# A graph network's attention steps on one core: weight pieces staged in pairs, late rows' parts asked for earlier, a difference moved to VectorE

## The chip, the core and the metric

The kernel runs on one core of one Trainium2 chip. The core has a matrix engine (TensorE, PE in the profile, with its weight loads as PEld), VectorE (DVE), ScalarE (ACT), GpSimd (POOL) and SyncE (SP), whose queue issues most DMAs. The metric is the time of one execution on the device in microseconds, the median of several runs. The profile is of one further execution.

## What is computed

1024 nodes of 512 features, 16 graphs of 64 nodes with 256 condition vectors each, 4 layers of attention and a gated feed-forward part between two graph convolutions:

```python
def _attn(xf, cond, Wq, Wk, Wv, Wo):
    q = (xb @ Wq).reshape(BS, -1, H, DH)
    k = (cond @ Wk).reshape(BS, -1, H, DH)
    v = (cond @ Wv).reshape(BS, -1, H, DH)
    att = jnp.einsum('bnhd,bmhd->bhnm', q, k) * DH ** (-0.5)
    w = jax.nn.softmax(att, axis=-1)
    o = jnp.einsum('bhnm,bmhd->bnhd', w, v).reshape(BS, -1, H * DH)
    return (o @ Wo).reshape(n, d)
...
h = (x - mu) * jax.lax.rsqrt(var + EPS) * bn_w + bn_b
h = _gcn(h, src, dst, gcn_in_w, gcn_in_b, n)
for i in range(L):
    a = _attn(_ln(h, ln2_w[i], ln2_b[i]), cond, Wq[i], Wk[i], Wv[i], Wo[i])
    h = h + a
    u = _ln(h, ln3_w[i], ln3_b[i]) @ geglu_w[i] + geglu_b[i]
    val, gate = jnp.split(u, 2, axis=-1)
    f = val * jax.nn.gelu(gate, approximate=False)
    h = h + f @ ffo_w[i] + ffo_b[i]
h = _gcn(h, src, dst, gcn_out_w, gcn_out_b, n)
return h + x_in
```

## The kernel before

**Products in three parts.** Large products are made of operands with few bits. An operand x is split in three: a high part (x scaled, rounded by ScalarE), a low part (what is left, by VectorE) and a third, their difference (by VectorE or GpSimd). A unit of a product (class `Twelve`, L352) is twelve matmuls of 128 by 512 into one PSUM bank: `begin` runs high by high and low by low, eight matmuls, and then ScalarE multiplies the bank in place (L373); `end` adds the four matmuls of the third parts and copies the bank out (L378 on VectorE, L380 on ScalarE). Units are staggered: another unit begins between a unit's `begin` and its `end`, so that ScalarE has that long for its scaling. There are eight PSUM banks.

**The attention loop** (from L1659) runs g over six of a layer's eight pairs of graphs. In a step the four key units of pair g + 1 run first, then the probabilities of pair g are transposed (`mix`, L882) and multiplied with its values (`po`, L866), while the first value unit of pair g + 1 begins; ScalarE writes the high part `oh` of the result (L890). Then come the scores of pair g + 1 (L823), their maxima on VectorE (L832), the exponentials on ScalarE (L843), the remaining value units, and the output product of pair g (`attn_out`, L904). Layer 0 also transposes and splits the condition blocks; later layers load their parts (`load_parts`, L283).

**Staged weights.** During these steps `staged(l)` (L943) prepares weight columns for the feed-forward part. It handles four column blocks j. Each is loaded (`fetch`, into tiles of a pool of six, of which the output weights hold four) and divided into pieces of 128 by 256: four for j = 0 and 1, seven sums and differences for j = 2 and 3. `stage` (L934) sends a piece through a staging buffer: high part on ScalarE (L938), low and third on VectorE (L939, L940), and a store to DRAM (L941). There are two such buffers (tag `gs2`). `staged` is a generator; each `next(staging)` in the loop places its next stretch at that point, behind all that ScalarE and VectorE have been given so far (`behind_traced`). Before the change a stretch is a whole block of four pieces, or three and four of the seven, at up to three places per step: behind the second key unit's begin, behind the first value unit's end, and at the end of step 3.

**The start of the feed-forward part** (from L1774). The rows of the last two pairs of graphs come late. Their normalised rows are transposed (L1844, L1845), written by both VectorE (L808) and ScalarE (L810), and then split (`split_late`, `split_right`, L1749 to L1761) for the second half of the plain columns (`half_1`). `ln3_sums` (L1605 to L1607) and `ln3_last_sum` (L1612) make sums and differences of row blocks for a Strassen-like scheme, whose parts follow in `late_parts` (L1861 to L1866). `ready[0]` is the first staged chunk: `begin_first` and `end_first` make its first product, `steps` the others, with sums on VectorE (L1160, L1185).

Within an engine the order is fixed when the program is built; names in rows such as `gs2_1_2_5` read: tile, layer 1, column block 2, piece 5. `k_1_5_2` is key unit 2 of layer 1's pair 5.

Of the kernel before, what the change touches and what calls it, by code (L numbers as in the profile page):

```python
# [18 lines left out]
P = 128  # L19
# [7 lines left out]
def gnn_kernel(  # L27
# [26 lines left out]
    nc = tc.nc  # L54
# [888 lines left out]
    def staged(l):  # L943
# [16 lines left out]
            return [of[:, i * M:(i + 1) * M] for of in tiles for i in range(2)]  # L960

        def split(j, pieces):
            if j < 2:
                for k, x in enumerate(pieces):
                    stage(x, half_dram[j, k], f"{l}_{j}_{k}")
                yield
                return
            a11, a21, a12, a22 = pieces
            name = f"{l}_{j}"
            s1, s2 = (rows.tile([P, M], F32, tag="gy", name=f"gy{i}_{name}", bufs=2)  # L970
                      for i in range(2))

            def put(x, i):
                stage(x, chunk_dram[j - PLAIN, SPLIT.index(i)], f"{name}_{i}")

            nc.vector.tensor_tensor(s1, a21, a22, OP.add)
            put(a22, 3)
            nc.vector.tensor_tensor(s2, s1, a11, OP.subtract)
            put(s1, 4)
            nc.vector.tensor_tensor(a21, a11, a21, OP.subtract)  # L980
            put(a11, 0)
            yield
            put(a21, 6)
            put(a12, 1)
            nc.vector.tensor_tensor(a12, a12, s2, OP.subtract)
            put(s2, 5)
            put(a12, 2)
            yield

        for j in range(KC):  # L990
            pieces = fetch(j)
            yield
            flow = split(j, pieces)
            for some in range(1 if j < PLAIN else 2):
                if some:
                    yield
                with behind_traced(mybir.EngineType.DVE, mybir.EngineType.Activation):
                    next(flow)

    class HalfWeights:  # L1000

# [490 lines left out]
    for l in range(L):  # L1492
# [103 lines left out]
        def ln3_turn(nb, by=(0, 1), each=lambda ins: ins):  # L1596
            turn(xns.pop(nb), ln3T[nb // 4], nb % 4 * P, LN3W + l * KC, LN3B + l * KC,
                 f"ln3_{l}_{nb}", by, each)
# [60 lines left out]
        for g in range(NG - 2):  # L1659
# [7 lines left out]
            for i, u in enumerate(k):  # L1667
                u.begin()
                if not i:
                    for end in ends:  # L1670
                        end()
                if i > 1:
                    k[i - 2].end()
                if i == 1 and g > 2:
                    next(staging, None)
                next(wo_flow, None)
            k[-2].end()
            for _ in wo_flow:
# [14 lines left out]
                split_cond(g + 2, None if g else scores.last)  # L1693
            v[1].begin()
            v[0].end()
            if g in (2, 3, 4):
                next(staging)
            v[2].begin()
            v[1].end()
            pieces = attn_out(l, g, oT, wo, pin)  # L1700
# [10 lines left out]
                scale_kept()  # L1711
            if l == 0 and g + 3 < NG:
                turn_cond(g + 3, each=pin)
            if g == 3:
                next(staging)
            if g == NG - 3:
                add_bias(nc.vector, *range(4))
# [50 lines left out]
        def split_late(at):  # L1768
            flows = [split_right(i, x, at) for i, x in late]
            for _ in range(2):  # L1770
                for flow in flows:
                    next(flow, None)
# [42 lines left out]
        with in_order(mybir.EngineType.DVE):  # L1815
# [27 lines left out]
            units[3].begin()  # L1843
            ln3_turn(g - 1, (1, 1), pin)  # L1844
            ln3_turn(g, (0, 0), pin)  # L1845
            units[2].end()
            ready[0].begin_first()
            units[3].end()
            split_late(slice(2 * P, 4 * P))
            ready[0].begin(1)  # L1850
            ready[0].end_first()
            ln3_sums(nc.vector, g - 1, g)
            ln3_last_sum(nc.gpsimd, g - 3, g - 2)
            ln3_last_sum(nc.gpsimd, g - 1, g)
        Chunk.rights[2] = rights[2]
# [29 lines left out]
        def fill(n=1):  # L1885
            for _ in range(n):
                next(parts, None)

        units = half_1(0) + half_1(1)
        units[0].begin()  # L1890
        fill(3)
        units[1].begin()
        units[0].end()
# [228 lines left out]
```

## Time and profile before

| | us |
|---|---|
| median of 3 runs | 2274.92 |
| lowest and highest run | 2270.91, 2276.71 |
| the profiled execution, its whole time | 2275.67 |
| the profiled execution, its span | 2273.9 |
| busy: VectorE, ScalarE, GpSimd | 1718.2, 1156.8, 506.6 |

The mean granted clock of TensorE in that execution is 0.997 of full speed. A row of the timeline has the start in us from the span's start, the time to the end of the row's last instruction, the engine, the line, the operation, the tiles written and read, the shapes, the count, and in brackets the idle time before it with what ended it. A row of the list of waits has who waited for whom, and then the total in us, the number of waits and the longest. A row of a window has its bounds, its length, the busy time of each engine with its number of instructions, the granted clock, the DMA share and GB/s. SPq is SP's DMA queue.

### The profile page before, as it was taken

What the parts mean: (1) busy time and instruction counts of PE and PEld (TensorE: products, weight loads), DVE (VectorE), ACT (ScalarE), POOL (GpSimd) and SP (SyncE); (2) the same over time, 40 slices, a digit from 0 to 9 for tenths busy, and PEclk for the clock granted to TensorE, in tenths of its full rate; (3) what the DMA queues carried; (4) which work ended last, traced back from release to release, by engine and by line L of the source; (5) the groups of instructions that cost most, each with busy time, mean ns of one, the idle gap of its engine ahead of it and who ended that gap; (6) DMA issues with size and microseconds to landing.
All of it is one profiled execution on the core that took longest, in us unless ns stands there. A gap on an engine that the chain in (4) does not pass through costs nothing. (4 is left out here: it accounts for less than half of the span.)

```text
span 2273.9 us, 35755 instructions
## 1 busy us (share of the span) xinstructions
PE 2240.1 (99%) x12768; PEld 1809.2 (80%) x12768; DVE 1718.2 (76%) x3296; ACT 1156.8 (51%) x2313; POOL 506.6 (22%) x487
## 2 busy tenths in 40 slices
PE   8999999999999999999999999999999999999999
PEld 5678878887888878888888887878888887878787
DVE  9886577999965466899975456899976466899965
ACT  7555555565354445565345445555436445566521
POOL 1122101485000000287000000178100000068301
PEclk9999999999999999999999999999999999999999
DMA  6154564434525264443534265443543346353551
GB/s 171 57 185 167 188 217 166 144 121 148 166 79 191 87 250 158 146 127 98 192 120 169 93 211 182 128 146 103 182 161 135 126 158 216 112 165 111 181 183 54
DMA packets 216953, 340.84 MB, mean 150 GB/s; under 512 B 16488, under 2 KB 117168, under 8 KB 216768
## 3 DMA queue, kind: packets, MB, share of 16 engines
q1 hardware_dynamic: 214672, 333.05, 43.2%
q0 software_dynamic: 1376, 4.30, 0.5%
q8 instruction: 105, 1.72, 0.3%
q10 hardware_dynamic: 720, 1.11, 0.1%
q14 instruction: 80, 0.66, 0.1%
HBM read 236.69 MB, written 101.72 MB: 149 GB/s over the span
## 5 line engine op out<-in xcount | busy, mean ns | idle before, releaser
L1154 ACT ACTIVATE g<-g 128x512 f32<-128x512 f32 x224 | 131.3, 586 | 185.9 <-PE g L1140 183.7
L1612 POOL TENSOR_TENSOR ln3T<-ln3T,ln3T 128x512 f32<-128x512 f32 x8 | 13.2, 1650 | 892.2 <-DVE ln3S L1605 892.2
L1319 PE MATMUL fy<-bl_wff,al_f 128*128 128x512 f32 x512 | 158.8, 390 | 0.0
L1319 PE MATMUL fx<-bs_wff,as_f 128*128 128x512 f32 x512 | 158.6, 390 | 0.0
L1319 PE MATMUL fy<-bh_wff,ah_f 128*128 128x512 f32 x512 | 157.7, 389 | 0.0
L304 ACT ACTIVATE ah_f<-fr 128x1024 fp32r<-128x1024 f32 x64 | 67.8, 1060 | 173.0 <-DVE al_f L305 81.7
L373 ACT ACTIVATE k<-k 128x512 f32<-128x512 f32 x125 | 73.1, 586 | 157.9 <-PE k L362 157.6
L843 ACT ACTIVATE pr<-sc,nmax 128x256 f32<-128x256 f32 x256 | 118.4, 473 | 40.6 <-DVE nmax L832 40.5
L832 DVE TENSOR_REDUCE nmax<-sc 128x2 f32<-128x512 f32 x128 | 83.6, 678 | 70.6 <-PE sc L823 70.6
L373 ACT ACTIVATE v<-v 128x512 f32<-128x512 f32 x127 | 74.7, 588 | 111.8 <-PE v L362 111.8
L1084 POOL TENSOR_TENSOR gsa<-gha,gla 128x512 fp32r<-128x512 f32 x96 | 122.6, 1299 | 19.8 <-DVE gla L1079 19.8
L1140 PE MATMUL g<-gr,gha 128*128 128x512 f32 x384 | 118.2, 389 | 0.0
L362 PE MATMUL v<-bs_wv,cs 128*128 128x512 f32 x384 | 104.6, 396 | 8.9 <-ACT v L373 8.9
L1319 PEld LDWEIGHTS fy<-bl_wff,al_f 128*128 128x128 f32 x512 | 96.1, 188 | 21.7 <-DVE bl_wff L1296 1.7
L1319 PEld LDWEIGHTS fx<-bs_wff,as_f 128*128 128x128 f32 x512 | 96.1, 188 | 21.4 <-DVE bs_wff L1300 1.7
L1319 PEld LDWEIGHTS fy<-bh_wff,ah_f 128*128 128x128 f32 x512 | 96.1, 188 | 19.8
L362 PE MATMUL v<-bh_wv,ch 128*128 128x512 f32 x384 | 107.9, 403 | 0.0
L362 PE MATMUL k<-ch,bh_wk 128*128 128x512 f32 x384 | 104.0, 393 | 0.0
L305 DVE SCALAR_TENSOR_TENSOR al_f<-ah_f,fr 128x1024 fp32r<-128x1024 f32 x64 | 78.1, 1221 | 34.2 <-ACT ah_f L304 28.1
L362 PE MATMUL v<-bl_wv,cl 128*128 128x512 f32 x384 | 103.2, 390 | 0.0
L362 PE MATMUL k<-cl,bl_wk 128*128 128x512 f32 x384 | 102.8, 389 | 0.0
L362 PE MATMUL k<-cs,bs_wk 128*128 128x512 f32 x384 | 101.4, 395 | 0.0
(333 smaller groups left out, 5951.4 us busy)
## 6 DMA issues: line engine op xcount, KB each, us to landing
f_dram<-fT SPq DMA_DIRECT2D x128, 256.0 KB, 2.1
fr<-f_dram SPq DMA_DIRECT2D x64, 512.0 KB, 4.6
ch<-cond_dram SPq DMA_DIRECT2D x48, 512.0 KB, 4.7
cl<-cond_dram SPq DMA_DIRECT2D x48, 512.0 KB, 6.2
cs<-cond_dram SPq DMA_DIRECT2D x48, 512.0 KB, 7.3
chunk_dram<-gs SPq DMA_DIRECT2D x56, 384.0 KB, 2.6
wff<-in_L_gnn_ffo_w_dram SPq DMA_DIRECT2D x32, 512.0 KB, 5.3
half_dram<-gs SPq DMA_DIRECT2D x32, 384.0 KB, 2.9
```

Of the source, the lines that this page charges most:

```text
L304: nc.scalar.mul(twelve_bits(h), x, INWARD * TINY)
L305: left_parts.low = nc.vector.scalar_tensor_tensor(twelve_bits(l), h, -1.0 / TINY, x, OP.mult, OP.add)
L362: pin(nc.tensor.matmul(self.bank, twelve_bits(left[k // 2])[:, k % 2, self.c * P:(self.c + 1) * P], twelve_bits(right[k // 2])[:, k % 2, : ...
L373: nc.scalar.mul(self.bank, self.bank, 1.0 + TINY)
L832: nc.vector.tensor_reduce(nmax[u], banks[u].rearrange("p (a m) -> p a m", a=2), AX.X, OP.max, negate=True)
L843: nc.scalar.activation(pr3[:, a, :], ps3[:, a, :], AF.Exp, bias=nmax[u][:, a:a + 1], accum_out=tot[:, a:a + 1])
L1084: split_left.last = pin(t.tensor_tensor(s_at, h_at, l_at, OP.subtract))
L1140: pin(nc.tensor.matmul(to, self.part(i, which)[:, k, :], self.rights[i][which].bitcast(F32R)[:, k, :], start=start and k == 0, stop=stop a ...
L1154: pin(nc.scalar.mul(to, to, 1.0 + TINY))
L1319: pin(nc.tensor.matmul(to, twelve_bits(left[which][0])[:, k, b * P:(b + 1) * P], twelve_bits(right[which])[:, k, :], start=u == 0 and whic ...
L1612: t.tensor_tensor(b12, b22, b12, OP.subtract)
```

## The change

Three edits, in every layer:

- `staged` gives its pieces in pairs (`islice(flow, 2)`), at four places of a step: behind the begin of the second and of the fourth key unit, behind the first value unit's end, and at the step's end. The 22 pieces of a layer now start at the end of step 2 and end in step 5. Each pair's arithmetic is otherwise the same; within blocks 2 and 3 the sums stand beside the pieces that they serve.
- `split_late` for the late rows stands right behind the last transposes instead of behind the last unit of the first half; `end_first` stands behind the begin of the second half's first unit.
- the late rows' third difference (`ln3_sums`, third) is made on VectorE instead of GpSimd.

```diff
@@ -960,10 +960,10 @@
             return [of[:, i * M:(i + 1) * M] for of in tiles for i in range(2)]
 
         def split(j, pieces):
-            if j < 2:
+            if j < PLAIN:
                 for k, x in enumerate(pieces):
                     stage(x, half_dram[j, k], f"{l}_{j}_{k}")
-                yield
+                    yield
                 return
             a11, a21, a12, a22 = pieces
             name = f"{l}_{j}"
@@ -975,27 +975,30 @@
 
             nc.vector.tensor_tensor(s1, a21, a22, OP.add)
             put(a22, 3)
+            yield
+            put(s1, 4)
+            yield
             nc.vector.tensor_tensor(s2, s1, a11, OP.subtract)
-            put(s1, 4)
             nc.vector.tensor_tensor(a21, a11, a21, OP.subtract)
             put(a11, 0)
             yield
             put(a21, 6)
+            yield
             put(a12, 1)
+            yield
             nc.vector.tensor_tensor(a12, a12, s2, OP.subtract)
             put(s2, 5)
+            yield
             put(a12, 2)
             yield
 
         for j in range(KC):
-            pieces = fetch(j)
-            yield
-            flow = split(j, pieces)
-            for some in range(1 if j < PLAIN else 2):
-                if some:
-                    yield
+            flow = split(j, fetch(j))
+            for _ in range(2 if j < PLAIN else 4):
+                yield
                 with behind_traced(mybir.EngineType.DVE, mybir.EngineType.Activation):
-                    next(flow)
+                    for _ in islice(flow, 2):
+                        pass
 
     class HalfWeights:
 
@@ -1671,8 +1674,8 @@
                         end()
                 if i > 1:
                     k[i - 2].end()
-                if i == 1 and g > 2:
-                    next(staging, None)
+                if i % 2 and g > 2:
+                    next(staging)
                 next(wo_flow, None)
             k[-2].end()
             for _ in wo_flow:
@@ -1693,8 +1696,8 @@
                 split_cond(g + 2, None if g else scores.last)
             v[1].begin()
             v[0].end()
-            if g in (2, 3, 4):
-                next(staging)
+            if g > 1:
+                next(staging, None)
             v[2].begin()
             v[1].end()
             pieces = attn_out(l, g, oT, wo, pin)
@@ -1711,7 +1714,7 @@
                 scale_kept()
             if l == 0 and g + 3 < NG:
                 turn_cond(g + 3, each=pin)
-            if g == 3:
+            if 1 < g < NG - 3:
                 next(staging)
             if g == NG - 3:
                 add_bias(nc.vector, *range(4))
@@ -1843,13 +1846,12 @@
             units[3].begin()
             ln3_turn(g - 1, (1, 1), pin)
             ln3_turn(g, (0, 0), pin)
+            split_late(slice(2 * P, 4 * P))
             units[2].end()
             ready[0].begin_first()
             units[3].end()
-            split_late(slice(2 * P, 4 * P))
             ready[0].begin(1)
-            ready[0].end_first()
-            ln3_sums(nc.vector, g - 1, g)
+            ln3_sums(nc.vector, g - 1, g, third=nc.vector)
             ln3_last_sum(nc.gpsimd, g - 3, g - 2)
             ln3_last_sum(nc.gpsimd, g - 1, g)
         Chunk.rights[2] = rights[2]
@@ -1888,6 +1890,7 @@
 
         units = half_1(0) + half_1(1)
         units[0].begin()
+        ready[0].end_first()
         fill(3)
         units[1].begin()
         units[0].end()
```

ScalarE in layer 1, from the copy of the keys in step 4 to the exponentials of pair 5, before the change:

```order
L380 COPY kT_1_5_1_22492<-k_1_5_2_22477 128x512
L882 COPY pT_1_4_0_22532<-tr_pr_1_4_0_22527 128x512
L938 ACTIVATE gs2_1_2_1_22455<-gx_1_2_1_22348 128x256
L882 COPY pT_1_4_2_22546<-tr_pr_1_4_2_22541 128x512
L938 ACTIVATE gs2_1_2_5_22461<-gy1_1_2_22406 128x256
L373 ACTIVATE v_1_5_0_22560<-v_1_5_0_22560 128x512
L938 ACTIVATE gs2_1_2_2_22466<-gx_1_2_1_22348 128x256
L890 ACTIVATE oh_1_4_22602<-po_1_4_22526 128x512
L843 ACTIVATE pr_1_5_0_22630,tot_1_5_0_22631<-sc_1_5_0_22606,nmax_1_5_0_22626 128x256 x2
```

The same place of the changed kernel, from just behind that copy:

```order
L938 ACTIVATE gs2_1_2_5_22493<-gy1_1_2_22406 128x256
L882 COPY pT_1_4_0_22521<-tr_pr_1_4_0_22516 128x512
L882 COPY pT_1_4_2_22535<-tr_pr_1_4_2_22530 128x512
L373 ACTIVATE v_1_5_0_22549<-v_1_5_0_22549 128x512
L890 ACTIVATE oh_1_4_22591<-po_1_4_22515 128x512
L843 ACTIVATE pr_1_5_0_22619,tot_1_5_0_22620<-sc_1_5_0_22595,nmax_1_5_0_22615 128x256 x2
L843 ACTIVATE pr_1_5_1_22629,tot_1_5_1_22630<-sc_1_5_1_22596,nmax_1_5_1_22617 128x256 x2
L843 ACTIVATE pr_1_5_2_22639,tot_1_5_2_22640<-sc_1_5_2_22597,nmax_1_5_2_22625 128x256 x2
L843 ACTIVATE pr_1_5_3_22647,tot_1_5_3_22648<-sc_1_5_3_22598,nmax_1_5_3_22635 128x256 x2
L373 ACTIVATE v_1_5_1_22657<-v_1_5_1_22657 128x512
L380 COPY v_1_5_0_22671<-v_1_5_0_22549 128x512
L938 ACTIVATE gs2_1_2_2_22674<-gx_1_2_1_22348 128x256
```

Pieces 1, 5 and 2 of block 2 stood between the key copy and `oh`; now piece 5 alone stands there, ahead of the transposed probabilities, and piece 2 behind the exponentials; piece 1 stands ahead of the key copy, outside these rows.

VectorE in layer 1 at the late rows, before the change:

```order
L808 TENSOR_SCALAR ln3T_1_1_1_23098<-tr_ln3_1_6_23690,cols_85 128x128 x2
L1047 SCALAR_TENSOR_TENSOR fT_1_0_1_23723<-g0_1_0_1_23680,gcols_86,gg_1_0_1_23475 128x512
L1751 SCALAR_TENSOR_TENSOR gr_1_7_1_23469<-ln3T_1_1_0_23097,gr_1_7_0_23468 128x2x256
L1751 SCALAR_TENSOR_TENSOR gr_1_2_1_23472<-ln3T_1_1_1_23098,gr_1_2_0_23471 128x2x256
L1761 SCALAR_TENSOR_TENSOR gr_1_7_2_23470<-gr_1_7_0_23468,gr_1_7_1_23469 128x2x256
L1761 SCALAR_TENSOR_TENSOR gr_1_2_2_23473<-gr_1_2_0_23471,gr_1_2_1_23472 128x2x256
L1605 TENSOR_TENSOR ln3S_1_0_23099<-ln3T_1_1_0_23097,ln3T_1_0_0_23095 128x2x256
L1606 TENSOR_TENSOR ln3S_1_1_23100<-ln3T_1_1_1_23098,ln3S_1_0_23099 128x2x256
L1864 SCALAR_TENSOR_TENSOR gl_1_5_23760<-ln3S_1_1_23100,gr_1_5_23758 128x512
```

The same place of the changed kernel:

```order
L808 TENSOR_SCALAR ln3T_1_1_1_23098<-tr_ln3_1_6_23690,cols_85 128x128 x2
L1754 SCALAR_TENSOR_TENSOR gr_1_7_1_23469<-ln3T_1_1_0_23097,gr_1_7_0_23468 128x2x256
L1754 SCALAR_TENSOR_TENSOR gr_1_2_1_23472<-ln3T_1_1_1_23098,gr_1_2_0_23471 128x2x256
L1764 SCALAR_TENSOR_TENSOR gr_1_7_2_23470<-gr_1_7_0_23468,gr_1_7_1_23469 128x2x256
L1764 SCALAR_TENSOR_TENSOR gr_1_2_2_23473<-gr_1_2_0_23471,gr_1_2_1_23472 128x2x256
L1050 SCALAR_TENSOR_TENSOR fT_1_0_1_23729<-g0_1_0_1_23680,gcols_86,gg_1_0_1_23475 128x512
L1608 TENSOR_TENSOR ln3S_1_0_23099<-ln3T_1_1_0_23097,ln3T_1_0_0_23095 128x2x256
L1609 TENSOR_TENSOR ln3S_1_1_23100<-ln3T_1_1_1_23098,ln3S_1_0_23099 128x2x256
L1610 TENSOR_TENSOR ln3S_1_2_23101<-ln3T_1_0_1_23096,ln3S_1_1_23100 128x2x256
L1866 SCALAR_TENSOR_TENSOR gl_1_5_23760<-ln3S_1_1_23100,gr_1_5_23758 128x512
```

The four instructions of the late parts stand ahead of the product `fT` of the last unit, and the difference `ln3S_1_2` has come in behind the other two sums.

ScalarE in layer 1 at the second half's first units, before the change:

```order
L1177 COPY gs1_1_0_2_23737<-g0_1_0_2_23713 128x512
L373 ACTIVATE g1_1_1_0_23748<-g1_1_1_0_23748 128x512
L1861 ACTIVATE gr_1_5_23758<-ln3S_1_1_23100 128x512 x2
L373 ACTIVATE g0_1_1_0_23772<-g0_1_1_0_23772 128x512
L1861 ACTIVATE gr_1_6_23767<-ln3T_1_1_0_23097 128x512 x2
L1044 ACTIVATE gg_1_1_0_23746<-g1_1_1_0_23748,gcols_86 128x512
L1861 ACTIVATE gr_1_23821<-ln3S_1_2_23101 128x512
L373 ACTIVATE g1_1_1_1_23804<-g1_1_1_1_23804 128x512
```

The same place of the changed kernel:

```order
L373 ACTIVATE g1_1_1_0_23744<-g1_1_1_0_23744 128x512
L1180 COPY gs1_1_0_2_23754<-g0_1_0_2_23719 128x512
L1863 ACTIVATE gr_1_5_23758<-ln3S_1_1_23100 128x512 x2
L1863 ACTIVATE gr_1_23821<-ln3S_1_2_23101 128x512
L1863 ACTIVATE gr_1_6_23767<-ln3T_1_1_0_23097 128x512 x2
L373 ACTIVATE g0_1_1_0_23772<-g0_1_1_0_23772 128x512
L1047 ACTIVATE gg_1_1_0_23742<-g1_1_1_0_23744,gcols_86 128x512
L1863 ACTIVATE gr_1_23821<-ln3S_1_2_23101 128x512
L1863 ACTIVATE gr_1_4_23791<-ln3S_1_0_23099 128x512 x2
L373 ACTIVATE g1_1_1_1_23804<-g1_1_1_1_23804 128x512
```

Five first parts of the late sums (`gr_1_5` twice, `gr_1`, `gr_1_6` twice) stand ahead of the scaling of the second unit (`g0_1_1_0`), where two stood.

## The prediction

> **What bounds the kernel now.** I read the page first, then the list of waits of TensorE, then its timeline at each wait, and last the timelines of the engines it waited for.
>
> ```profile
> span 2273.9 us, 35755 instructions
> PE 2240.1 (99%) x12768; PEld 1809.2 (80%) x12768; DVE 1718.2 (76%) x3296; ACT 1156.8 (51%) x2313; POOL 506.6 (22%) x487
> PE v L362 <- ACT v L373: 12.6, 6, 3.5
> PE g L1140 <- DVE g L1160: 2.7, 4, 0.8
> PE g L1140 <- DVE gl L1864: 0.4, 2, 0.2
> ```
>
> TensorE (PE) is busy for 2240.1 of 2273.9 us, so no other engine can give time back except by ending a wait of TensorE. The change touches no matmul's size, only orders. What it can win lies in three of these lines: 12.6 us in which the last third of a value unit waits for ScalarE to scale its bank (L373), and 2.7 + 0.4 us at the start of the feed-forward part, where TensorE waits for VectorE. The profiled execution took 2275.67 us, 1.8 us more than its span; the median of the three runs is 2274.92 us, 0.75 us below it. The sum is made against 2275.67.
>
> The wait rows hide a part of the loss, so I take whole steps of the attention loop. The first value matmuls behind the scores of step g + 1 mark one step each; layer 0 first, then 1, 2 and 3.
>
> ```profile
> 245.50 1.20 PE L362 MATMUL v<-bh_wv,ah_c 128*128 128x512 f32 x4
> 277.79 1.20 PE L362 MATMUL v<-bh_wv,ah_c 128*128 128x512 f32 x4
> 311.02 1.20 PE L362 MATMUL v<-bh_wv,ah_c 128*128 128x512 f32 x4
> 347.89 1.20 PE L362 MATMUL v<-bh_wv,ah_c 128*128 128x512 f32 x4
> 806.17 1.20 PE L362 MATMUL v<-bh_wv,ch 128*128 128x512 f32 x4
> 836.66 1.20 PE L362 MATMUL v<-bh_wv,ch 128*128 128x512 f32 x4
> 871.61 1.20 PE L362 MATMUL v<-bh_wv,ch 128*128 128x512 f32 x4
> 1359.92 1.20 PE L362 MATMUL v<-bh_wv,ch 128*128 128x512 f32 x4
> 1396.74 1.20 PE L362 MATMUL v<-bh_wv,ch 128*128 128x512 f32 x4
> 1886.02 1.20 PE L362 MATMUL v<-bh_wv,ch 128*128 128x512 f32 x4
> 1919.57 1.20 PE L362 MATMUL v<-bh_wv,ch 128*128 128x512 f32 x4
> ```
>
> An undisturbed step is 277.79 - 245.50 = 32.29 us in layer 0, which also transposes its condition blocks, and 836.66 - 806.17 = 30.49 us in layers 1 to 3. The step behind the scores of g = 5 is 36.87, 34.95, 36.82 and 33.55 us: **4.58, 4.46, 6.33 and 3.06 us too long, 18.43 us together**. Layer 0 also loses 0.94 us one step earlier (33.23 us).
>
> Why that step? ScalarE and VectorE in layer 1, in order of time:
>
> ```profile
> 823.32 0.42 ACT L938 ACTIVATE gs<-gx 128x256 fp32r<-128x256 f32 x1 [3.06 <-DMA gx<-in_L_gnn_geglu_w_dram]
> 827.58 0.42 ACT L938 ACTIVATE gs<-gx 128x256 fp32r<-128x256 f32 x1 [1.88 <-DMA chunk_dram<-gs]
> 829.61 0.59 ACT L882 COPY pT<-tr_pr 128x512 f32<-128x512 f32 x1
> 837.54 0.42 ACT L938 ACTIVATE gs<-gx 128x256 fp32r<-128x256 f32 x1 [2.50 <-DMA chunk_dram<-gs]
> 837.87 0.58 ACT L890 ACTIVATE oh<-po 128x512 fp32r<-128x512 f32 x1
> 838.79 1.28 DVE L832 TENSOR_REDUCE nmax<-sc 128x2 f32<-128x512 f32 x2
> 843.45 0.59 ACT L373 ACTIVATE v<-v 128x512 f32<-128x512 f32 x1
> 844.10 1.60 PE L362 MATMUL v<-bs_wv,cs 128*128 128x512 f32 x4 [2.61 <-ACT v L373]
> ```
>
> A weight piece goes through one of two staging buffers: ScalarE writes its first third (L938), VectorE the other two, and a store empties the buffer. The seventh piece in a row, at 837.54, waited 2.50 us for a store to land. Both engines work in order, so behind it stand the attention output's first part (oh) and, on VectorE, the maxima of the scores. These begin at 838.79, although the scores ended near 836.7; the eight exponentials and then the bank's scaling (843.45) slide with them, and TensorE stands still for 2.61 us. One step earlier, with fewer pieces, the same scaling came in time:
>
> ```profile
> 810.08 0.59 ACT L373 ACTIVATE v<-v 128x512 f32<-128x512 f32 x1
> 810.84 1.09 PE L362 MATMUL v<-bs_wv,cs 128*128 128x512 f32 x4
> ```
>
> It ended at 810.67, 0.17 us ahead of the matmul at 810.84. That is the whole margin: once the stall is gone, this chain of maxima, exponentials and scaling is next, and whatever stands ahead of it by more than 0.17 us comes back one for one.
>
> **Pieces in pairs.** The number of pieces, of their instructions and of their DMAs stays. What moves is where they stand. Up to the transposes of g = 4, the pieces of column block 2 now come two behind g = 3's end, two behind the second key unit and two behind the fourth; the last, the one of 837.54, stands behind the exponentials and the copy of the value block. So oh and the maxima find nothing in front. Does each pair find free buffers there? Six intervals between the seven pieces took 837.54 - 823.32 = 14.2 us, 2.4 us each, 4.7 us per pair. The new places lie 20 matmuls apart, about 4.3 us (21 took 4.40 us in the second window row below), so the pairs just keep pace, and they start earlier: the load that held 823.32 back for 3.06 us is asked for one place sooner. I put the first pair near 819. The last piece ahead of the transposed probabilities falls near 829, beside the copy at 829.61, which TensorE first needs here:
>
> ```profile
> 832.76 2.08 PE L866 MATMUL po<-pT,v 128*64 128x64 f32 x64
> ```
>
> 829.61 + 0.59 leaves 2.56 us of cover; without it a late store would cost what exceeds 2.56 us. On SP's queue the stores now stand ahead of four of the six loads of the next condition block (ch, cl, cs). Those are used a step later, and most of its 30.49 us covers them; without this cover a late load costs its delay. I take this part as the whole 18.43 us. In layer 0 the condition's own splitting, which stretches the step by 0.94 us, stays where it is in the step of g = 4's scores; I leave that loss in.
>
> Behind a stall the matmuls are slow for a while, and the granted clock (the third number from the end) says why:
>
> ```profile
> 844.00:848.60 4.60, 4.50 (x13) 3.54 (x14) 4.57 (x12) 1.78 (x5) 0.00 (x0) 0.63 0.93 374
> 848.60:853.00 4.40, 4.40 (x21) 3.61 (x20) 2.18 (x5) 1.49 (x3) 0.00 (x0) 1.00 0.35 135
> 318.60 1.73 PE L362 MATMUL v<-bs_wv,as_c 128*128 128x512 f32 x4 [2.75 <-ACT v L373]
> 1368.28 2.07 PE L362 MATMUL v<-bs_wv,cs 128*128 128x512 f32 x4 [3.52 <-ACT v L373]
> ```
>
> The clock was 0.63 in the 4.60 us behind layer 1's stall and 1.00 again after that. The step's loss less the stall is this tail: 4.58 - 2.75 = 1.83 us in layer 0, 4.46 - 2.61 = 1.85 in layer 1, 6.33 - 3.52 = 2.81 in layer 2. I count them as owed to the stall, so they go with it. The Trainium skill ("TensorE: Matmul & The Clock Gate", Part 1) says that the clock halves after an idle window of about 3.4 us, whose bounds run freely. By that rule only layer 2's stall is long enough; the trace, with tails behind 2.61 and 2.75 us, does not agree.
>
> **Late rows and the difference.** In layer 1:
>
> ```profile
> 937.76 10.14 PE L1025 MATMUL g<-gr,gp 128*128 128x512 f32 x44
> 936.68 0.75 DVE L1047 SCALAR_TENSOR_TENSOR fT<-g,gcols,gg 128x512 f32<-128x512 f32 x1 [1.77 <-PE g L1025]
> 941.86 1.00 DVE L1864 SCALAR_TENSOR_TENSOR gl<-ln3S,gr 128x512 fp32r<-128x512 f32 x1 [0.70 <-ACT gr L1861]
> 942.90 1.67 DVE L1866 SCALAR_TENSOR_TENSOR gs<-gr,gl 128x512 fp32r<-128x512 f32 x1
> 945.21 0.69 DVE L1866 SCALAR_TENSOR_TENSOR gs<-gr,gl 128x512 fp32r<-128x512 f32 x1
> 942.28 1.74 POOL L1607 TENSOR_TENSOR ln3S<-ln3T,ln3S 128x512 f32<-128x512 f32 x1
> 942.26 0.58 ACT L373 ACTIVATE g<-g 128x512 f32<-128x512 f32 x1
> ```
>
> VectorE idles 1.77 us for fT, and from 942.90 on it works nearly without a gap up to the sums of L1160, for which TensorE waits. The four instructions of the late parts now stand ahead of fT and wait for ScalarE's first parts alone, so they fill a part of that idle time: between 0 and 1.77 us, I take 0.7. The difference on VectorE costs 0.69 us (the row at 945.21 has its shape and two like operands), but GpSimd's 1.74 us go, beside which the row at 942.90 took 1.67 instead of 0.69 us: 0.98 us back. The difference fills the 0.70 us wait at 941.86, so VectorE is some 0.7 + 0.98 = 1.7 us ahead and stays so, against waits of TensorE of 0.2 to 0.8 us. So **the 2.7 + 0.4 = 3.1 us go**. The third part of unit 0 that moves behind the next unit's start costs nothing: the same two matmuls, covered by the eight put before them.
>
> The bounds. On ScalarE five first parts, not two, now stand ahead of the second unit's scaling, which was done at 942.26 + 0.58 = 942.84. Three more at 0.58 us, less the 0.7 us, put it at 943.9. Its matmul is the 29th of the 44 from 937.76: 937.76 + 28 x 10.14 / 44 = 944.2. So 0.3 us of cover; should the parts come late for want of the difference, I estimate at most 0.5 us at each of two units in four layers: 4 us. The other end is a gain: the 0.94 us of layer 0. I take 0.
>
> **Sum.** 2275.67 - 18.43 - 3.1 = 2254.1, so **2254 us**, 0.9% below; the terms' ends give 2253 to 2258.
>
> **The rivals.**
> - *Only half the attention stalls go.* Two buffers and six pieces ahead of the scores remain; if the pairs jam again, oh comes late by half. 2275.67 - 9.2 - 3.1 = 2263. For it: the jam was one of stores, and they stay. Against: the piece that jammed is behind the exponentials now.
> - *The tails are not the stalls'.* If the slow clock behind the stalls of 2.75 and 2.61 us has another cause, 3.7 us stay: 2258. Against: they begin exactly at the stall. The Trainium skill's rule above would give this.
> - *The change does not reach the stall.* The scaling stays late from the condition's splitting and the maxima alone: only 3.1 us go, 2272.6. Against: layer 1 has no splitting and stalls all the same.
> - *Slower.* Three pieces per layer now stand right ahead of the transposed probabilities. If their stores land later than the cover of 2.56 us allows, by about 2.5 us, TensorE stops at three places in four layers: 12 x 2.5 = 30 us against 21.5 won, 2284. It decides from 21.5 / 12 = 1.8 us per place on. For it, a store that took 819.36 - 814.1 = 5 us:
>
> ```profile
> 813.60 0.89 SPq L941 DMA_DIRECT2D half_dram<-gs  x2
> 819.36 0.42 ACT L938 ACTIVATE gs<-gp 128x256 fp32r<-128x256 f32 x1 [2.04 <-DMA half_dram<-gs]
> ```
>
> Against it: the stores around it freed their buffers within the 4.7 us of a pair.
>
> **How the numbers follow.** Forecast 0.74; half 0.11; tails 0.05; not reached 0.05; slower 0.05. A measurement of this kernel tells 0.3%, 6.8 us, from no change, so faster means below 2268.1: 0.74 + 0.11 + 0.05 = 0.90, of which I move 0.02 to the same for terms that fail together. Same 0.07, slower 0.05. The range reaches from the lower end, 2253, less the 4.0 us by which the lowest of the three runs lies below their median, to the half case, without which it would hold less than 8 in 10: 2249 to 2264.
>
> **What would show it.** Right: the list of waits has no wait of v for L373 above 1 us, the step behind the scores of g = 5 takes 30.5 us (32.3 in layer 0), the granted clock stays 1.0 there, no wait of g for the sums of L1160 above 0.2 us, and VectorE's instruction of the row at 942.90 takes 0.7 us. Wrong: waits of po for pT, of k for its scaling, or of the first feed-forward units for L373.

## The result and the profile after

The changed kernel took **2255.14 us** (median of 4 runs, 2254.72 to 2257.01), the kernel before 2274.3 beside it (2270.91 to 2276.71): ratio 0.9918, 95% interval 0.9901 to 0.9936. The profiled execution took 2254.72 us. Its page begins:

```profile
span 2252.9 us, 35754 instructions
PE 2232.4 (99%) x12768; PEld 1805.2 (80%) x12768; DVE 1718.0 (76%) x3300; ACT 1157.8 (51%) x2313; POOL 500.5 (22%) x483
```

GpSimd has 6.1 us less to do (the four differences), VectorE and ScalarE the same to 1 us. TensorE's busy time is 7.7 us shorter at the same number of matmuls; most of it will be the slow ones behind the stalls, whose tails made 6.8 us. The lines of the list of waits (total, number, longest in us) that answer to those of before:

```profile
PE v L362 <- ACT v L373: 0.9, 2, 0.6
PE g L1028 <- ACT g L373: 0.5, 3, 0.2
PE g L1143 <- DVE g L1163: 0.2, 1, 0.2
```

12.6 us have become 0.9, both waits of layer 0, and the waits for VectorE's sums at the start of the feed-forward part are gone (the 0.2 is one of layer 1, later). The middle line is new, and it is one of the signs of being wrong that the prediction named: the second of the feed-forward units waits for its scaling, by 0.15 us in each of the four layers (one of the four is a little too short for the list). Where the 21.0 us of the span come from, worked out from the starts of TensorE's rows (a step from one group of scores to the next; the feed-forward part's start from its first half-product, L1025 before and L1028 after, to the first output product):

| layer | step behind g = 5, before | after | start of feed-forward, before | after |
|---|---|---|---|---|
| 0 | 36.87 | 32.61 | 161.73 | 161.06 |
| 1 | 34.95 | 30.52 | 161.26 | 161.26 |
| 2 | 36.82 | 30.52 | 162.23 | 161.01 |
| 3 | 33.55 | 30.52 | 162.21 | 161.04 |
| gain | | 18.02 | | 3.06 |

Layer 1 gains nothing at its feed-forward start: its wait of 0.34 us for a sum is gone, but one of 0.15 us for the scaling and one of 0.25 us for a later sum have come.

ScalarE and TensorE in layer 1, as the timeline has them: the row of pieces, the attention output's first part (oh), the bank's scaling, the matmul that waited for it, and the two groups of scores that bound the step.

```profile
815.30 0.42 ACT L938 ACTIVATE gs<-gx 128x256 fp32r<-128x256 f32 x1 [2.96 <-DMA gx<-in_L_gnn_geglu_w_dram]
...
824.32 0.42 ACT L938 ACTIVATE gs<-gx 128x256 fp32r<-128x256 f32 x1 [1.96 <-DMA chunk_dram<-gs]
825.63 0.42 ACT L938 ACTIVATE gs<-gy 128x256 fp32r<-128x256 f32 x1 [0.42 <-DMA chunk_dram<-gs]
830.12 0.60 ACT L890 ACTIVATE oh<-po 128x512 fp32r<-128x512 f32 x1 [1.38 <-PE po L866]
835.80 0.59 ACT L373 ACTIVATE v<-v 128x512 f32<-128x512 f32 x1
836.57 1.09 PE L362 MATMUL v<-bs_wv,cs 128*128 128x512 f32 x4
830.00 1.96 PE L823 MATMUL sc<-kT,qT 64*64 64x256 f32 x32
860.52 0.66 PE L823 MATMUL sc<-kT,qT 64*64 64x256 f32 x8
831.00:840.00 9.00, 9.00 (x55) 7.00 (x48) 7.78 (x21) 5.69 (x20) 0.00 (x0) 1.00 0.74 267
```

Pieces still wait for stores (1.96 and 0.42 us), but the last of them ahead of oh is done at 826.05, and oh waits for TensorE, no longer the other way round. The scaling ends at 836.39, the matmul at 836.57 finds it done: again 0.18 us of margin, as in an undisturbed step. The window's granted clock (1.00) has no tail.

At the start of the feed-forward part, layer 1, VectorE, GpSimd, ScalarE and TensorE:

```profile
930.51 0.69 DVE L1609 TENSOR_TENSOR ln3S<-ln3T,ln3S 128x512 f32<-128x512 f32 x1
931.24 1.67 DVE L1610 TENSOR_TENSOR ln3S<-ln3T,ln3S 128x512 f32<-128x512 f32 x1
930.62 1.74 POOL L1615 TENSOR_TENSOR ln3T<-ln3T,ln3T 128x512 f32<-128x512 f32 x1 [4.54 <-DVE ln3S L1608]
933.55 0.69 DVE L1868 SCALAR_TENSOR_TENSOR gs<-gr,gl 128x512 fp32r<-128x512 f32 x1
933.00 0.63 ACT L1863 ACTIVATE gr<-ln3S 128x512 fp32r<-128x512 f32 x1 [0.61 <-DVE ln3S L1610]
934.58 0.58 ACT L373 ACTIVATE g<-g 128x512 f32<-128x512 f32 x1
935.21 0.98 PE L1028 MATMUL g<-gr,gp 128*128 128x512 f32 x3 [0.15 <-ACT g L373]
```

The third part (L1868) takes 0.69 instead of 1.67 us, as foretold. But now the difference itself (L1610) takes 1.67 instead of 0.69: GpSimd had two instructions of 1.74 us at this place, and the one that stayed (L1615, one of the other sums) runs beside it. ScalarE waits 0.61 us for it ahead of the second unit's scaling, and TensorE then 0.15 us for that.

### The profile page after: what moved, and what is told of

Its sections match the earlier page's. It is cut to its first block, busy times and chain, and to the rows that moved or that the text cites. A ratio compares the mean times of both kernels' runs of the same rounds, so it can differ in the third digit from the quotient of the medians.

```text
span 2252.9 us, 35754 instructions
## 1 busy us (share of the span) xinstructions
PE 2232.4 (99%) x12768; PEld 1805.2 (80%) x12768; DVE 1718.0 (76%) x3300; ACT 1157.8 (51%) x2313; POOL 500.5 (22%) x483
## 3 DMA queue, kind: packets, MB, share of 16 engines
q10 hardware_dynamic: 720, 1.11, 0.1%
## 5 line engine op out<-in xcount | busy, mean ns | idle before, releaser
L1615 POOL TENSOR_TENSOR ln3T<-ln3T,ln3T 128x512 f32<-128x512 f32 x8 | 13.2, 1654 | 875.2 <-DVE ln3S L1608 875.2
L305 DVE SCALAR_TENSOR_TENSOR al_f<-ah_f,fr 128x1024 fp32r<-128x1024 f32 x64 | 78.1, 1221 | 33.6 <-ACT ah_f L304 27.5
```

The source lines that it names most:

```text
L305: left_parts.low = nc.vector.scalar_tensor_tensor(twelve_bits(l), h, -1.0 / TINY, x, OP.mult, OP.add)
```

## The experiments

**The two parts alone.** `e1_pairs_only` undoes the late rows and the difference, `e2_late_only` keeps the staging of before:

```diff
 # e1, against the change
-            split_late(slice(2 * P, 4 * P))
             units[2].end()
...
+            split_late(slice(2 * P, 4 * P))
             ready[0].begin(1)
-            ln3_sums(nc.vector, g - 1, g, third=nc.vector)
+            ready[0].end_first()
+            ln3_sums(nc.vector, g - 1, g)
```

> The pairs alone; late rows and difference as before the change. My theory, two gains that do not touch each other: the attention part gives 18.0 us, the waits at the start of the feed-forward part stay at about 3.1 us, so some 2257 us, and the step behind the scores of g = 5 takes 30.5 us in layers 1 to 3. Rival, the parts lean on each other (the late rows' order gives a share of the attention gain, or the pairs a share of the other): a time above 2262, or one within 1 us of the changed kernel's 2255.

> Late rows and difference as in the change; the staging as before it. My theory: only the 3.1 us of waits at the start of the feed-forward part go, 2271 us, and all four long waits of the value units for their scaling (2.6 to 3.5 us each) stay, with matmuls at a slow clock behind some of them. Rival, the parts lean on each other: below 2268.

Measured: pairs alone 2257.1 us (ratio 0.9921, 0.9904 to 0.9937), late rows alone 2271.07 (0.9976, 0.9964 to 0.9988). Both theories hold in their times. In the traces the first has steps of 30.52 us and still 2.6 us of waits for the sums, the second has the four long waits (2.16 to 3.99 us, where 2.6 to 3.5 were expected) and a start of the feed-forward part of 160.97 to 161.05 us in every layer.

**What cured the stall: pairs, place or number?** The prediction gave two reasons, that the pairs just keep pace with the stores and that oh has nothing in front. `e6_last_piece_ahead` keeps the pairs, but takes the third place ahead of the transposes:

```diff
+            if g > 1:
+                next(staging, None)
             v = values(l, g + 1, wv)
             oT = mix(l, g, probs, vs.pop(g), (k[-1].end, v[0].begin))
...
-            if g > 1:
-                next(staging, None)
```

`e8_one_piece_moved` is the kernel before with the seventh piece of block 2 behind the first value unit, `e10_two_pieces_moved` the same with the sixth too; block 3 follows a place later. The edit of e10 (in e8 the `yield` stands ahead of `put(a12, 2)`):

```diff
             put(a12, 1)
+            if j == PLAIN:
+                yield
...
-            for some in range(1 if j < PLAIN else 2):
+            for some in range(1 if j < PLAIN else 3 if j == PLAIN else 2):
...
-            if g == 3:
+            if g in (3, 4):
                 next(staging)
```

`e5_three_buffers` is the kernel before with `bufs=3` for the staging buffers, and 34 instead of 35 tiles in the pool of slots.

> The changed kernel with the third place of a step moved from behind the first value unit's end to ahead of the transposes, so that the last piece of block 2 stands right ahead of the attention output's first part again, as it did before the change; the loads are still asked for earlier and the pairs stay. My theory, what counts is the pace of two buffers from the first piece on (2.4 us a piece): the pieces start near 820 instead of 823, the seventh falls near 834.5, just before the output is ready, and at most 1 us per layer is lost: 2255 to 2259. Rival, what counts is that a piece stands ahead of that output at all: the waits of 2.6 to 3.5 us are back and with them 18 us, about 2272.

> The kernel before, with one of the 22 pieces moved: the last piece of column block 2 stands behind the first value unit's end, where it falls behind the exponentials, instead of in front of the attention output's first part; the pieces of block 3 follow one place later. Everything else comes in stretches of three and four as before. Theory (place, not pairing): the four long waits of v for its scaling go with their tails, 18.4 us, and the feed-forward part keeps its waits: 2275.6 - 18.4 = 2257.2, the step behind the scores of g = 5 30.5 us (32.5 in layer 0). Rival (a stretch of three in a row still fills both buffers, and the exponentials stay late by half): 2266. Second rival (the stall moves one step on, to block 3's pieces, which now start later): 2270 or more.

> The kernel before with the last two pieces of column block 2 moved behind the first value unit's end, all else in stretches of three and four. Theory of the row: five pieces stand ahead of the attention output's first part; the fifth begins about 21.5 + 4 x 2.4 = 31.1 us at the latest behind the start of the scores of g = 4 and was at 29.8 with one piece moved, so layers 1 to 3 lose their waits: 13.9 us. In layer 0 VectorE still has piece 1 and the difference for piece 2 ahead of the maxima, and about half of the loss stays: 2274.5 - 13.9 - 2 = 2258.6, between 2257 and 2261. Rival (pairs are needed, since stretches of three and four fill both buffers): as with one piece moved, 2266.

> The kernel before with three staging buffers instead of two (one tile less for the slots, to make room). Theory of the row of seven: a piece may begin when the store two (now three) pieces back has landed, so seven pieces take 14 us with two buffers, and oh, ready about 30.6 us behind the start of the scores of g = 4, is held back when the seventh stands ahead of it and begins later than that. With three buffers the pace falls from 2.4 to about 1.6 us, the seventh begins about 19 + 6 x 1.6 = 28.6 us, and in layers 1 to 3 the long waits of v for its scaling go: 4.5 + 6.3 + 3.1 = 13.9 us. Layer 0's stays, since there VectorE's own work on pieces 1 and 5, slowed beside GpSimd, holds the maxima back and no store: 2274.5 - 13.9 = 2260.6. Rival (the stores, not the buffers, are slow: the loads of the condition blocks on the same queue hold them up): at most half goes, 2267 or more. Rival (layer 0 has the same cause): 2256.5.

Measured: e6 2272.08 us (0.9993, 0.9981 to 1.0005), e8 2265.77 (0.9967, 0.9955 to 0.998), e10 2259.96 (0.9939, 0.9925 to 0.9953), e5 2269.28 (0.9981, 0.9969 to 0.9992). In e6 and e8 the theory fell; their times are those of a rival, but their traces show other reasons than the rival gave. e10 came out as its theory had it, and e5 has the time of its first rival and, as shown below, the steps of its theory. ScalarE in layer 1 of e6, with the matmul that waits:

```profile
839.73 0.42 ACT L938 ACTIVATE gs<-gx 128x256 fp32r<-128x256 f32 x1 [2.17 <-DMA chunk_dram<-gs]
840.05 0.58 ACT L890 ACTIVATE oh<-po 128x512 fp32r<-128x512 f32 x1
846.28 1.21 PE L362 MATMUL v<-bs_wv,cs 128*128 128x512 f32 x4 [0.67 <-ACT v L373]
```

And of e8:

```profile
838.53 0.42 ACT L938 ACTIVATE gs<-gy 128x256 fp32r<-128x256 f32 x1 [2.84 <-DMA chunk_dram<-gs]
838.85 0.58 ACT L890 ACTIVATE oh<-po 128x512 fp32r<-128x512 f32 x1
845.09 1.20 PE L362 MATMUL v<-bs_wv,cs 128*128 128x512 f32 x4 [1.35 <-ACT v L373]
```

In e6 the seventh piece stands in front of oh and waits for a store, pairs or not. In e8 the seventh is out of the way, and the sixth waits in its place. These stalls are much shorter than before, though. In the profiled executions layer 0 makes up about half of what e6 loses to the changed kernel in the attention steps, and most of what e8 loses there. e6 moves the third place of every step, so it stalls one step earlier too, and layers 1 to 3 lose 1.6 to 2.2 us each; layer 0's step behind the scores of g = 4 alone takes 39.18 instead of 33.14 us, with this wait:

```profile
286.91 2.07 PE L362 MATMUL v<-bs_wv,as_c 128*128 128x512 f32 x4 [3.00 <-ACT v L373]
```

e6's profiled execution is the fastest of its ten (2268.12 us); where its median has 4 us more is not shown. In e8 the waits of layers 1 to 3 are 1.35, 0.39 and 0 us, while layer 0's step behind the scores of g = 5 is 38.18 us, longer than before. That its time is that of the rival with half the stall is luck.

In layer 1 all six kernels follow one count. Block 2's pieces form a row that starts when its columns have landed and goes on, in the main, at one piece per freed buffer; oh could begin 30.6 us behind the start of the scores of g = 4, and is late when the last piece ahead of it is. In layer 1, in us from the start of those scores (an L823 row):

| kernel | row starts | pieces ahead of oh | last of them starts | us per piece | oh starts | wait of v |
|---|---|---|---|---|---|---|
| before | 19.0 | 7 | 33.3 | 2.4 | 33.6 | 2.61 |
| e6 | 17.5 | 7 | 32.4 | 2.5 | 32.7 | 0.67 |
| e8 | 19.3 | 6 | 32.0 | 2.5 | 32.3 | 1.35 |
| e10 | 19.0 | 5 | 27.5 | 2.1 | 30.6 | none |
| after | 15.8 | 6 | 26.1 | 2.1 | 30.6 | none |
| e5 | 18.2 | 7 | 26.3 | 1.4 | 30.6 | none |

So it is not pairing as such. The change starts the row 3.2 us earlier, since two of block 1's four pieces now stand a place earlier, so that it gives up its tiles sooner (block 2's last load is asked for 10.3 instead of 16.4 us behind the scores), and it has one piece fewer ahead of oh. An early row also meets faster stores: in the kernel before, the row's first three stores land 2.3 us after their issue, the next three after 3.3, 4.2 and 5.4 us. Those stand among loads of the next condition block on the same queue; whether the loads slow them is not shown, since no run moves the loads alone. Either a shorter row (e10) or a third buffer (e5) ends the stalls of layers 1 to 3 as well: the steps of e5 there,

```profile
844.03 1.96 PE L823 MATMUL sc<-kT,qT 64*64 64x256 f32 x32
874.56 0.66 PE L823 MATMUL sc<-kT,qT 64*64 64x256 f32 x8
```

are 30.53 us. e5 is slow elsewhere, ahead of all staging: its second group of scores starts at 188.37 us, before's at 179.01. Less these 9.4 us, which the missing slot may cost (no run has the missing slot alone), its profiled execution of 2270.71 us would be 2261.3, the theory's 2260.6.

**Layer 0 has another cause.** e5 and e10 keep a wait in layer 0 (3.67 and 2.15 us), which the count of stores doesn't explain. VectorE, GpSimd and ScalarE there, in the kernel before:

```profile
308.62 1.41 DVE L940 TENSOR_TENSOR gs<-gs 128x256 fp32r<-128x256 f32 x1
309.95 1.49 DVE L985 TENSOR_TENSOR gx<-gx,gy 128x256 f32<-128x256 f32 x1
...
312.95 1.40 DVE L940 TENSOR_TENSOR gs<-gs 128x256 fp32r<-128x256 f32 x1
314.27 1.28 DVE L832 TENSOR_REDUCE nmax<-sc 128x2 f32<-128x512 f32 x2
308.47 2.69 POOL L313 TENSOR_TENSOR as_c<-ah_c,al_c 128x512 fp32r<-128x512 f32 x2 [27.86 <-PE po L866]
312.71 2.79 POOL L313 TENSOR_TENSOR as_c<-ah_c,al_c 128x512 fp32r<-128x512 f32 x2 [1.55 <-issue]
315.92 0.42 DVE L940 TENSOR_TENSOR gs<-gs 128x256 fp32r<-128x256 f32 x1
313.22 0.42 ACT L938 ACTIVATE gs<-gx 128x256 fp32r<-128x256 f32 x1 [2.91 <-DMA chunk_dram<-gs]
314.99 0.48 ACT L843 ACTIVATE pr<-sc,nmax 128x256 f32<-128x256 f32 x1 [1.35 <-DVE nmax L832]
```

No row of VectorE waits for a store. ScalarE's seventh piece does, behind oh, but the exponentials behind it wait 1.35 us more for the maxima, so VectorE decides. It is busy without a gap up to the maxima, which begin 4.1 us later than in the changed kernel (38.4 against 34.3 us behind the scores of g = 4; the step is 4.3 us longer): the parts of pieces 1 and 5 take 1.4 us instead of 0.42 beside GpSimd's third parts of the condition. With piece 5 and the difference for piece 2 moved behind the maxima, the wait falls from 4.07 (e8) to 2.15 us (e10). In e5 other staging work stands there, the first sums of block 3 (L976, L978). In the changed kernel pieces 1 and 5 and the difference are done ahead of the stretch, piece 2 comes behind the maxima, and VectorE waits for the scores again. The long step of e6's layer 0 looks alike: up to the maxima VectorE has no gap, and an L940 takes 1.39 us beside GpSimd.

**The start of the feed-forward part.** Three kernels take late rows, difference and ScalarE's order apart. `e4_pairs_and_diff` puts the late rows back and keeps the difference on VectorE; `e3_diff_on_pool` the other way round (only `third=nc.vector` is taken out). `e7_scaling_first` is the changed kernel with ScalarE held to the written order at these units, and `e9_scaling_first_diff_on_pool` is e7 with the difference on GpSimd:

```diff
 # e7, against the change
-        units = half_1(0) + half_1(1)
-        units[0].begin()
+        with in_order(mybir.EngineType.Activation):
+            units = half_1(0) + half_1(1)
+            units[0].begin()
...
 # e9, besides
-            ln3_sums(nc.vector, g - 1, g, third=nc.vector)
+            ln3_sums(nc.vector, g - 1, g)
```

> Pairs and the difference on VectorE; the late rows' parts in their old place, behind the first half's last unit. With neither of the two the first unit sums of L1163 are waited for by 0.74, 0.34, 0.74 and 0.76 us. Theory A (GpSimd's other sum, L1615, still runs beside, so the difference takes about 1.67 us on VectorE and only 2.7 us of the 3.4 us chain to the first third part are saved: 0.3 us): the waits shrink to 0.44, 0, 0.44, 0.46, and the time is 2257.1 - 1.3 = 2255.8. Rival (the prediction's sizing, 1.7 us ahead by the difference alone): no wait is left, 2254.5. Second rival (the late rows do it all): 2257.1. In none of them does the second unit wait for its scaling, since two first parts stand ahead of it as before.

> The changed kernel with the late rows' third difference back on GpSimd. My theory: VectorE's lead falls from 1.7 to 0.7 us, against waits of 0.2 to 0.8 us per layer, so 0.3 to 0.8 us in all come back: 2255.5 to 2256; an instruction of 1.67 us beside GpSimd's shows up again on VectorE. Rival, the difference alone makes the gain there: 3 us come back, 2258.

> The changed kernel with ScalarE's order fixed at the second half's units: three groups of first parts, not five instructions, stand ahead of the second unit's scaling, and those of the difference behind it. Theory: the waits of 0.15 us per layer of the second unit for its scaling go, and nothing else moves: 2255.14 - 0.6 = 2254.5. Rival (the parts of the difference are then late for VectorE's third parts, and the sums of L1163 are waited for again, by up to 0.7 us per layer): 2258.

> As the kernel with ScalarE's order fixed, and the difference on GpSimd. Theory (what the difference on GpSimd cost with the late rows moved, 5 us, was ScalarE standing still 1.7 us for GpSimd's result ahead of the second unit's scaling, and nothing else): with the scaling ahead of those parts the four waits of 1.2 us go and the first third part is ready as early as in the kernel with late rows alone: 2260.1 - 4.9 = 2255.2, within 0.5 us of the changed kernel, so the move to VectorE is not needed. Rival (VectorE slowed beside GpSimd is late for the sums of L1163): waits of 0.3 to 0.8 us per layer there, 2257.

Measured: e4 2256.27 us (0.9926, 0.9898 to 0.9954), e3 2260.08 (0.9929, 0.9912 to 0.9945), e7 2253.88 (0.9915, 0.9887 to 0.9944), e9 2254.28 (0.9914, 0.9886 to 0.9942). e3 lost more than any theory gave it. ScalarE, GpSimd and TensorE in its layer 1:

```profile
933.71 1.16 ACT L1863 ACTIVATE gr<-ln3S 128x512 fp32r<-128x512 f32 x2
934.78 1.74 POOL L1610 TENSOR_TENSOR ln3S<-ln3T,ln3S 128x512 f32<-128x512 f32 x1
936.56 0.64 ACT L1863 ACTIVATE gr<-ln3S 128x512 fp32r<-128x512 f32 x1 [1.69 <-POOL ln3S L1610]
938.14 0.58 ACT L373 ACTIVATE g<-g 128x512 f32<-128x512 f32 x1
938.77 1.43 PE L1028 MATMUL g<-gr,gp 128*128 128x512 f32 x5 [1.23 <-ACT g L373]
```

The late rows' new place makes ScalarE's order put a first part of the difference ahead of the second unit's scaling. With the difference on GpSimd, ScalarE stands still 1.69 us for it, TensorE 1.23 us for ScalarE, in each of four layers: 4.9 us. In e9 the same difference on GpSimd costs 0.4 us against e7, within the scatter of the two (2253.0 to 2254.53 and 2253.24 to 2255.4), because the scaling goes first; one of its layers waits 0.58 us for the sums. So the difference's engine matters mainly through what ScalarE has queued behind it.

In e4 the difference alone brings the end of VectorE's first third part 0.38 us forward in layer 0 (23.41 instead of 23.79 us into the part, e4 against e1), about what theory A said. e4's time is near theory A's too, but the waits for the sums are not: 0.82, 0.82 and 0.81 us in three layers, where 0.44 to 0.46 were expected, and none in layer 1. VectorE and GpSimd in layer 0 of e4:

```profile
412.97 1.67 DVE L1610 TENSOR_TENSOR ln3S<-ln3T,ln3S 128x512 f32<-128x512 f32 x1
412.36 1.73 POOL L1615 TENSOR_TENSOR ln3T<-ln3T,ln3T 128x512 f32<-128x512 f32 x1 [5.29 <-DVE ln3S L1608]
424.80 1.23 DVE L1867 SCALAR_TENSOR_TENSOR gl<-ln3S,gr 128x512 fp32r<-128x512 f32 x1
426.06 1.11 DVE L1869 SCALAR_TENSOR_TENSOR gr<-gr,gl 128x512 fp32r<-128x512 f32 x1
425.56 2.22 POOL L1115 TENSOR_TENSOR gxa<-gxa 128x256 f32<-128x256 f32 x2
```

The 0.38 us won are given back 12 us later, beside GpSimd's column sums (L1115): the two rows take 1.23 and 1.11 instead of 0.7 us, while in e1 only the second does (1.12). The column sums begin when a load lands, and which rows they slow differs between layers and kernels. In layer 2 of the kernel before they begin early enough to slow the first of the two rows as well:

```profile
1478.53 1.24 DVE L1864 SCALAR_TENSOR_TENSOR gl<-ln3S,gr 128x512 fp32r<-128x512 f32 x1
1478.49 0.74 POOL L1112 TENSOR_TENSOR gxa<-gxa,gxb 128x256 f32<-128x256 f32 x1 [9.34 <-DMA gxa<-in_L_gnn_geglu_w_dram]
```

Layer 3 has the same, layer 0 has not (0.69 us). With the pairs alone (e1) neither layer 2 nor layer 3 has it, and they start in 161.64 and 161.66 instead of 162.23 and 162.21 us; e8 and e10 have it in one layer each. So, by e1, some 1.1 us of the 3.06 hang on when a load lands and not on the late rows or the difference. Of what VectorE itself gains, the late rows' place has the larger share: the first third part ends 23.04 us into the part with it and without the difference (e9) and 22.66 us with both (the changed kernel, and e7, so ScalarE's order does not move it), against 23.79 us with neither (e1). That is 0.75 us for the late rows and 0.38 us for the difference.

**A version faster than the change.** e7 was 1.3 us below the changed kernel, where its theory had 0.6. Both once more, on one chip:

> The changed kernel itself, beside the kernel with ScalarE's order fixed on the same chip. Expected 2255.1, with waits of 0.15 us per layer of the second unit for its scaling and a feed-forward start of 161.0 to 161.3 us.

> ScalarE's order fixed, beside the changed kernel on the same chip. Theory (the feed-forward part's start is 0.5 us shorter in each layer, as its trace had it: 160.5 us in three layers, 161.1 in one): 1 to 2 us below the changed kernel, outside the scatter of the two. Rival (the difference of 1.3 us in the medians was scatter of the prologue): within 0.5 us.

Measured: the change 2254.81 us (2254.26 to 2254.89, five runs), e7 2253.37 (2252.47 to 2254.1, five runs): 1.4 us less, without overlap. ScalarE in its layer 1:

```profile
932.28 1.15 ACT L1863 ACTIVATE gr<-ln3T 128x512 fp32r<-128x512 f32 x2
933.34 0.58 ACT L373 ACTIVATE g<-g 128x512 f32<-128x512 f32 x1
933.86 0.67 ACT L1047 ACTIVATE gg<-g,gcols 128x512 f32<-128x512 f32 x1
934.42 1.14 ACT L1863 ACTIVATE gr<-ln3S 128x512 fp32r<-128x512 f32 x2
```

The scaling ends 22.5 us into the part instead of 23.6, the four waits of 0.15 us are gone, and the part starts in 160.6 us in two layers (its theory had three); in the other two 0.19 us of waiting for the sums come back (161.1). A short wait costs more than its length: the start takes 160.5 to 160.6 us in the layers of e7 that wait for nothing in the list, and 161.0 to 161.1 us in those of the changed kernel with the one wait of 0.15 us. That fits e7's winning more than its theory's 0.6 us.

## Why the prediction was right, step by step

- **The attention stalls, 18.43 us foretold, 18.02 measured.** The step lengths of 30.5 us (in layer 0 32.61 instead of 32.3), the clock of 1.00 and the missing waits came as written. The reason given was right for layers 1 to 3 (a piece that waits for a store in front of oh), but half of it was loose: "the pairs just keep pace" says little, since e6 has the pairs and a stall. What decides is when the row starts and how many pieces of it stand ahead of oh. The sketch of that row held: foretold from 819 to 829, found from 815.30 to 825.63 in a kernel that is 4.77 us ahead at this point (scores of g = 4 at 799.51 instead of 804.28), so 820.1 to 830.4. Block 2's load was not asked for a place sooner, as the prediction has it; it stands at the same place, with two pieces fewer ahead of it. For **layer 0 the reason was wrong**: there VectorE, slowed beside GpSimd, held the maxima back, much as the rival "the change does not reach the stall" had it. That its 4.58 us went too (4.26 measured) was luck: the same edit happened to remove that work.
- **Layer 0's 0.94 us stay**: its step behind the scores of g = 4 is 33.14 us (33.23 before), its wait 0.6.
- **The tails** were counted with the stalls, and left with them.
- **3.1 us at the feed-forward part's start, 3.06 measured**, but the agreement is in part luck. The late rows' place brought 0.75 us, near the 0.7 put on it. The 0.98 us that GpSimd's absence was to give back moved from L1868 to the difference, as a second GpSimd instruction ran beside, and the difference brought 0.38. So VectorE is 1.13 us ahead and not 1.7, which was still more than the waits of 0.2 to 0.8 us. The 3.1 us of old waits went, but 0.85 us of new ones came, and some 1.1 us in layers 2 and 3 depend, by e1, on when GpSimd's column sums begin.
- **The cover of 0.3 us for the second unit's scaling** was 0.15 us short, a sign of being wrong that the prediction had named: 0.6 us in four layers by the list of waits, which e7 wins back and more. Its bound, 4 us if the parts came late, is what e3 met (4.9).
- **The slower rival** named the stores ahead of the transposed probabilities. No wait of po for pT is in the list of after; where stores were late in e6 and e8, oh paid, not pT.
- **The sum**: 2254.1 against 2254.72 for the profiled execution; the steps gave 0.4 us less, the prologue took 0.2 us more (the second group of scores at 179.23 instead of 179.01).

## What to carry to other kernels

When background work shares an in-order engine with the critical chain, count the row: its start, the pieces ahead of the critical instruction, the time per freed buffer; compare the last one's start with the moment that the chain needs the engine. A moved instruction carries its wait along, so look at what the scheduler then puts behind it (e3), and before crediting an engine with a neighbour's absence, list all that the neighbour still runs there (L1615).

## What the hardware showed

**A stall's tail doesn't follow its length.** Step's loss less stall, over the long waits of v in five traces (before, e2, e5, e8, e10): waits of 2.16, 2.59, 2.61, 2.75, 3.25, 3.67 and 4.07 us had tails of 1.8 us, 3.52 and 3.99 us of 2.8, and 2.15 and another 2.75 us of 0.3. The 0.3 us seems to go with any wait: e8's wait of 1.35 us cost 0.27 us more than its length. Windows behind the waits of 2.16 us (late rows alone, layer 3) and 2.15 us (e10, layer 0):

```profile
1892.70:1897.30 4.60, 4.58 (x13) 3.63 (x14) 4.57 (x12) 1.70 (x4) 0.00 (x0) 0.63 0.88 354
319.20:323.80 4.60, 4.53 (x20) 3.70 (x21) 3.58 (x9) 2.08 (x6) 0.00 (x0) 1.00 0.93 303
```

The granted clock was 0.63 behind one and 1.00 behind the other. The Trainium skill ("TensorE: Matmul & The Clock Gate", Part 1) puts the drop behind an idle window of about 3.4 us with free-running bounds; free bounds agree with such chance, the threshold does not, since 2.16 us were enough. Each stall thus adds a gamble: over all measurements the kernel before ranged over 13 us (2268.95 to 2282.2 in 49 executions), the changed one over 2.8 (2254.26 to 2257.01 in nine). The mean clock goes with it: 0.994 to 0.996 in the executions of the kernel before above 2278 us, 0.998 to 0.999 in those below 2270.

**VectorE and GpSimd exclude each other for whole instructions.** In the rows above L1610 of after ends at 932.91, GpSimd's L1615 at 932.36: 0.55 us behind; in e4 414.64 and 414.09, again 0.55; in layer 0 of before L985 ends at 311.44, GpSimd's pair at 311.16: 0.28 for half the size. VectorE's instruction, so it seems, stands until GpSimd's has ended and then runs for its own 0.69 (0.42) us less 0.14. The Trainium skill ("SBUF — State Buffer", Who interferes with whom) says that a VectorE instruction with two inputs in SBUF contends with a GpSimd instruction that reads SBUF, over a port pair that works as an exclusive lock; these rows agree.
